# An adaLN block with a mixture of experts: blocks of four sizes at the end, and a first chunk in two halves

## The chip, the cores and the metric

The kernel runs on one core of a Trainium2 chip. The metric is the device time of one execution in microseconds (us). A core has five engines that run their own instruction streams side by side: TensorE (PE in the profile; its weight loads are the row PEld), VectorE (DVE), ScalarE (ACT), GpSimd (POOL) and SyncE (SP), which here only issues transfers. They wait for each other through semaphores. All data is float32.

## The reference, cut to what matters

There are T = 4 x 1024 = 4096 tokens of D = 256 features. A modulation `mod`, one row of six parts for each of the four sequences, scales and shifts two layer norms and gates two residual branches. The first branch is a gated scan along the sequence, the second a mixture of 8 experts of which every token uses two.

```python
mod = (silu(c) @ wmod).reshape(4, 6, 1, 256)
sa, ca, ga, sb, cb, gb = (mod[:, i] for i in range(6))
ga, gb = at_least_a_quarter(ga), at_least_a_quarter(gb)     # keeps the sign
h = layernorm(x) * (1 + ca) + sa
# branch 1
xn = rms_scale * h / (norm(h) * 256 ** -0.5 + 1e-8) * split_scale
K = sigmoid(xn @ W_K)                                        # 256 -> 512
u, g_in, g_out = split(xn @ W_ugg, 3)                        # 256 -> 3 x 512
u = u * sigmoid(g_in) * (1 - K)
s = scan(s_t = K_(t-1) * s_(t-1) + u_t)                      # along the sequence
x = x + ga * ((s * sigmoid(g_out)) @ W_out + h)
# branch 2
h = layernorm(x) * (1 + cb) + sb
w = two best of softmax(h @ Wg + bg), scaled to sum 1
y = sum over the two experts e of
      w_e * (gelu(h @ W1[e] + b1[e]) @ W2[e] + b2[e])        # 256 -> 1024 -> 256
x = x + gb * y
```

## The kernel before, in words

The order of the instructions on every engine is written out by hand (the tile framework runs in manual schedule): what a function emits first is queued first, and each engine works its queue in order.

**The start** (lines 95 to 165, 200 to 312 and 988 to 1019). SP's queue takes `c`, then a third of `wmod`, the other two thirds, W_K, three parts of W_ugg, the second chunk of x, W_out and the third chunk. ACT's queue takes the first chunk of x (512 tokens, four tiles of 128), then the small vectors, `rms_sb` and `split_sb` among them. VectorE takes the mean and variance of the first chunk (`stats`, line 213; the power -0.5 on GpSimd), `shift` (226), ScalarE normalizes (`norm`, 232). TensorE multiplies a broadcast silu(c) with the first third of `wmod` into the bank `pm` (989). VectorE applies `1 + ca` and `sa` to the four tiles (996). ScalarE sums the squares (`a_square`, 364), `a_root` (375) and `a_scale` (380) make `u`, the tokens divided by their rms. TensorE turns `u` (1014), and ScalarE and VectorE, one half of the features each, bring it out of PSUM as `hT`, multiplied by `rs_sb`, the product of the two scale vectors (1015, 1016). `all_rows` (287) meanwhile makes the modulation of all four sequences, which `other_rows` (299) finishes and stores in DRAM as `rows`; from there later chunks read theirs as `mda` and `mdf`. `keep_busy(n)` (260) puts n transposes of the identity into TensorE's queue, whose result nothing reads; it is called with 14, 8 and 18.

**Stage A** (loop at line 1020) works through eight chunks of TB = 512 tokens. Each chunk has four calls of `project` (402), one for each 128 of the 512 columns, and each of these four products `pk`, `pgi`, `pu` and `pgo` of two matmuls over all 512 tokens (417), in four PSUM banks. The vector work of the previous and the next chunk is laid between them. After the scan comes the output projection (`o_pe`, 446), the second layer norm, and the gate (`f_gate`, 554): its weights are padded to 32 columns so that four products stand side by side in TensorE's columns. VectorE then picks the two best experts, and GpSimd scatters each token's number and weight to a list of its expert in DRAM (`drain`, 582).

**Stage B** works through blocks of TK = 256 entries of these lists. `b_up(j)` (917) multiplies the block's tokens `xT` by W1 (16 matmuls into banks `ph`, GELU by ScalarE into `g`), `b_down(j)` (952) multiplies `g` by W2, 128 tokens at a time into a bank `py` of eight matmuls; VectorE adds the bias and scales the rows (972, 973), and GpSimd adds them to their places in the output by an indirect DMA (`add_rows`, 944). `b_turn(j + 1)` (898) turns the next block's gathered rows on VectorE, between the two; it is 16 transposes of 32x32 squares, over two tiles or, with `half`, over one. Entries are fetched three blocks ahead, rows (gathers by GpSimd) and weights (two transfers of 1 MB) two ahead; weights lie in three places, of which every third is `proj` (line 114), once the projections' weights. While the routing is not complete, blocks come from partial tables; at block 8 VectorE makes the last table (`late_table`, 765, out of `blocks_of`, 700, and `table`, 709), which puts blocks of at most 128 tokens last.

Whatever the routing, at least 28 blocks are whole and at least 32 exist; these bounds are `sure_whole` and `sure`. So blocks 2 to 27 are emitted without a branch. Blocks 28 to 31 are a branch each, whole or half (128 tokens). From block 32 on, `rest` (1202) nests: if block j exists, add what the previous one kept, do block j, go on with j + 1, up to `NJ` = 39 possible blocks. A block from 31 on keeps its last part back in `last_y` and `last_at`, and the add comes at the start of the next `rest` or at the end:

```python
    def work_either(j, keep=False):
        with tc.If(n_whole > j) as whole:
            work(j, False, keep)
        with whole.Else():
            work(j, True, keep)

    def rest(j):
        with tc.If(n_blocks > j):
            add_rows(last_y, last_at, T)
            work_either(j, True)
            if j + 1 < NJ:
                rest(j + 1)
```

## Time and profile before

| | |
|---|---|
| median of the runs (3) | 790.62 us (790.05 to 791.95) |
| the profiled execution's own time | 789.1 us |
| its span, first to last instruction | 787.4 us |
| granted TensorE clock, mean | 0.997 |
| TensorE busy | 772.8 us (98%) |
| VectorE, ScalarE, GpSimd busy | 504.3, 241.7, 290.3 us |
| TensorE busy in 0 to 30 us | 27.82 us |
| TensorE busy in 30 to 400, 400 to 728 us | 368.06, 327.33 us |
| TensorE busy in 728 us to the end | 49.60 of 59.40 us |
| DMA share in 400 to 728 us | 0.81, 227 GB/s |

How to read the lines that the profile gives: L928 is line 928 of the kernel. A group's row names the line, the engine and the operation, then the tiles (output, then inputs), their shapes, and how many such instructions it holds; in a timeline two columns stand ahead, the start in us from the start of the span and the busy time, and in square brackets the idle time before the group with what ended it. `ph_False` and `pye_False` are the PSUM banks of a whole block's two products, `ph_True` and `pye_True` those of a half one. A matmul of float32 has two records here and a transpose one, so 16 matmuls are 32 records. Busy times come from the profiled execution alone.

### The profile page before, as it was taken

How to read it: one execution, taken by the hardware profiler on the slowest of the kernel's cores; microseconds unless marked ns; L12 is line 12 of the kernel's file. 1: busy time of each engine (PE TensorE's matmuls, PEld its weight loads, DVE VectorE, ACT ScalarE, POOL GpSimd, SP SyncE). 2: the span in 40 equal slices, each digit the busy share in tenths (PEclk: the TensorE clock that was granted, in tenths of full speed). 3: DMA queues.
4: the chain of work that ended last, by engine and by line, in shares of the span. 5: the costliest groups of instructions: out<-in, count | busy, mean ns of one | idle time of the engine just before them, and what ended most of it. 6: DMA issues, size and time to landing. Idle time of an engine off the chain costs nothing.

```text
span 787.4 us, 10804 instructions
## 1 busy us (share of the span) xinstructions
PE 772.8 (98%) x3279; PEld 577.1 (73%) x3279; DVE 504.3 (64%) x1391; ACT 241.7 (31%) x560; POOL 290.3 (37%) x370
## 2 busy tenths in 40 slices
PE   8999999999999999999999999999999999999995
PEld 5455545454546557888888888888888888888994
DVE  5787877898789869767547453544536354453563
ACT  4434243534433343223222122221312222131231
POOL 2102010106142712456564564634434243343431
PEclk9999999999999999999999999999999999999998
DMA  8321334042313265799469898898878687885781
GB/s 296 95 70 47 116 102 142 23 127 86 100 55 113 55 185 183 241 328 258 73 161 206 249 247 253 245 294 223 235 211 230 186 235 217 218 232 167 221 264 25
DMA packets 116040, 138.13 MB, mean 175 GB/s; under 512 B 25782, under 2 KB 100090, under 8 KB 115968
## 3 DMA queue, kind: packets, MB, share of 16 engines
q1 hardware_dynamic: 97184, 111.46, 45.0%
q0 software_dynamic: 17216, 25.25, 15.9%
q10 hardware_dynamic: 1568, 0.57, 0.3%
q8 instruction: 32, 0.52, 0.3%
q14 instruction: 40, 0.33, 0.1%
HBM read 113.52 MB, written 25.42 MB: 176 GB/s over the span
## 4 chain that ended last, share of the span: by engine, by line
PE 83%; DMA 8%; DVE 4%; issue 2%; POOL 1%; ACT 1%; POOLq 0%; DVEq 0%
PE ph_False L928 25%; PE pye_False L958 23%; PE pya L454 7%; PE pk L417 6%; PE pgi L417 6%; PE pu L417 6%; PE pgo L417 6%; DMA hb<-hx,ent 5%; DMA out_dram<-yb_False,ent 2%; PE idle L263 1%; DMA proj<-in_L_ffn_W_dram 1%; PE pm L290 1%; PE pta L399 1%; PE pl L564 1%; DVE s L443 0%
## 5 line engine op out<-in xcount | busy, mean ns | idle before, releaser
L937 ACT ACTIVATE g_False<-ph_False,bb 128x256 f32<-128x256 f32 x248 | 103.8, 470 | 303.0 <-issue 188.2
L915 DVE STREAM_TRANSPOSE xT<-hb 32x128 f32<-32x128 f32 (+1 forms) x576 | 168.8, 293 | 12.7 <-DMA hb<-hx,ent 3.6
L958 PE MATMUL pye_False<-w,g_False 128*128 128x256 f32 x672 | 148.7, 379 | 0.0
L928 PE MATMUL ph_False<-xT,w 128*128 128x256 f32 x672 | 148.6, 379 | 0.0
L928 PEld LDWEIGHTS ph_False<-xT,w 128*128 128x128 f32 x672 | 127.4, 190 | 17.9 <-issue 0.7
L958 PEld LDWEIGHTS pye_False<-w,g_False 128*128 128x128 f32 x672 | 127.5, 190 | 17.6 <-issue 0.2
L945 POOL DMA_INDIRECT out_dram<-yb_False,ent x46 | 73.4, 1595 | 139.9 <-DVE yb_False L973 138.4
L972 DVE TENSOR_TENSOR yb_False<-pye_False,b2b 128x256 f32<-128x256 f32 x42 | 17.8, 424 | 126.3 <-PE pye_False L958 123.8
L586 POOL DMA_INDIRECT lists<-pay,placei x64 | 66.4, 1037 | 38.5 <-DMA ent<-lists 27.4
L928 PE MATMUL ph_False<-xT,proj 128*128 128x256 f32 x320 | 70.8, 379 | 0.7 <-DMA proj<-in_L_ffn_W_dram 0.7
L958 PE MATMUL pye_False<-proj,g_False 128*128 128x256 f32 x320 | 70.7, 379 | 0.0
L928 PEld LDWEIGHTS ph_False<-xT,proj 128*128 128x128 f32 x320 | 60.7, 190 | 9.3 <-DVE yb_False L972 1.0
L958 PEld LDWEIGHTS pye_False<-proj,g_False 128*128 128x128 f32 x320 | 60.8, 190 | 8.3
L830 POOL DMA_INDIRECT hb<-hx,ent x53 | 55.6, 1048 | 22.4 <-issue 15.6
L417 PE MATMUL pk<-hT,proj 128*128 128x512 f32 x128 | 61.0, 599 | 0.7 <-ACT hT L1015 0.7
L223 POOL TENSOR_TENSOR rstd_f<-rstd_f,expo 128x4 f32<-128x4 f32 x8 | 8.2, 1022 | 142.4 <-DVE rstd_f L222 98.8
L417 PE MATMUL pu<-hT,proj 128*128 128x512 f32 x128 | 60.2, 592 | 0.0
L417 PE MATMUL pgo<-hT,proj 128*128 128x512 f32 x128 | 60.2, 592 | 0.0
L417 PE MATMUL pgi<-hT,proj 128*128 128x512 f32 x128 | 60.2, 592 | 0.0
L454 PE MATMUL pya<-wo,z 128*128 128x256 f32 x256 | 56.8, 380 | 0.0
L454 PEld LDWEIGHTS pya<-wo,z 128*128 128x128 f32 x256 | 48.4, 190 | 8.6 <-issue 2.4
L972 DVE TENSOR_TENSOR yb_False<-pye_False,wo_sb 128x256 f32<-128x256 f32 x20 | 8.5, 424 | 60.4 <-PE pye_False L958 60.3
(234 smaller groups left out, 811.1 us busy)
## 6 DMA issues: line engine op xcount, KB each, us to landing
w<-in_L_ffn_W_dram SPq DMA_DIRECT2D x48, 1024.0 KB
proj<-in_L_ffn_W_dram SPq DMA_DIRECT2D x24, 1024.0 KB
hx<-gb SPq DMA_DIRECT2D x4, 1024.0 KB
out_dram<-x SPq DMA_DIRECT2D x8, 512.0 KB
hx<-h SPq DMA_DIRECT2D x8, 512.0 KB
x<-in_L_attn_x_dram SPq DMA_DIRECT2D x7, 512.0 KB
swapped<-u SPq DMA_DIRECT2D x7, 512.0 KB
hT<-swapped SPq DMA_DIRECT2D x28, 128.0 KB
```

Of the source, the lines that this page charges most:

```text
L223: nc.gpsimd.tensor_tensor(rstd, rstd, expo[:, 0, :], ALU.pow)
L263: nc.tensor.transpose(idle[:, :P], ident, ident)
L417: nc.tensor.matmul(ps, lhsT=w[:, k, col : col + P], rhs=hT[:, k, :], start=(k == 0), stop=(k == KC - 1),)
L454: nc.tensor.matmul(py[:, t, :], lhsT=z[hc][:, ts(2 * q + t, P)], rhs=wo[:, hc, :], start=(hc == 0), stop=(hc == HC - 1),)
L586: ins = nc.gpsimd.indirect_dma_start(out=lists[:, :], out_offset=IndirectOffsetOnAxis(ap=place, axis=0), in_=what, in_offset=None, bounds_ ...
L830: nc.gpsimd.indirect_dma_start(out=hb[:, t, :], out_offset=None, in_=hx[: seen(j), :], in_offset=IndirectOffsetOnAxis(ap=BK[j]["ent"][:, t ...
L915: nc.vector.transpose(to[ts(q, SQ), :, :, ts(i, SQ)], hb[ts(i, SQ), :, :, ts(q, SQ)])
L928: nc.tensor.matmul(ph[:, u, :], lhsT=w1[:, k, ts(fc, P)], rhs=xT[:, k, :n], start=(k == 0), stop=(k == KC - 1),)
L937: nc.scalar.activation(g[:, fc, :n], ph[:, u, :], AF.Gelu_apprx_tanh, bias=bb[:, fc : fc + 1])
L945: return nc.gpsimd.indirect_dma_start(out=out_rows[:n], out_offset=IndirectOffsetOnAxis(ap=at, axis=0), in_=yb, in_offset=None, bounds_che ...
L958: nc.tensor.matmul(py, lhsT=g[:, fc, ts(t, P)], rhs=w2[:, fc, :], start=(fc == 0), stop=(fc == FC - 1),)
L972: nc.vector.tensor_add(yb, py, b2b)
```

## The change

**Sizes of blocks.** Blocks have one of four sizes, 256, 192, 128 and 64, instead of two. `late_table` counts, for each expert, how many blocks reach into each size, and puts all of one size before those of the next. For each size a count `n_upto` is loaded into registers. The bounds are worked out for each size (`sure(k)`): 26 blocks are whole in any case, 32 exist. So blocks 26 to 31 and the nested ones from 32 on choose among those sizes that are possible for their number, by branches inside each other's Else. Rows are fetched and turned in tiles of 128 as before (`half` is `size <= P`). The product up takes as many columns as the size; the product down takes the last part with 64 rows if the size leaves 64: its eight matmuls then go in turn to the lower and the upper 64 output partitions of the same bank, and VectorE adds the two halves of the bank with one more instruction. `last_y` is cleared once at the start by GpSimd, since a kept part of 64 rows is added with all 128. A temporary of the last table lies in the W_out tile.

**The first chunk.** Its first 256 tokens come by ACT's queue, the other 256 by SP's between the first and the second part of `wmod`. Statistics, normalization, modulation, squares, root, scaling and the turn are made for two tiles at a time. The first call of `project` makes its four products for the first 256 tokens, then turns the second half (ahead of the fourth product), then makes the four products of the second half into the same banks; `other_rows`, `load_mdf(0)`, the statistics of chunk 1 and its `shift` stand behind the second turn, in the middle of that call. The copies of silu(c) transposed, `scT` and its broadcast `scB`, go from VectorE to ScalarE, behind two transfers that ACT issues. The product `rs_sb` stands earlier on VectorE. The three copies of `all_rows` stand behind the first turn on ScalarE. `keep_busy` is called with 10 and 4, and no third time.

The core of the diff:

```diff
+    HT = TPB // 2
+    halves = [slice(i * HT, (i + 1) * HT) for i in range(2)]
+    X[0] = {"x": deep.tile([P, TPB, D], F32, tag="x", name="x_0", bufs=5)}
+    x0 = x[0].rearrange("(n p) d -> p n d", p=P)
     nc.sync.dma_start(out=c_sb, in_=c)
-    load_x(0, nc.scalar)
+    nc.scalar.dma_start(out=X[0]["x"][:, halves[0]], in_=x0[:, halves[0]])
     nc.sync.dma_start(out=wmod_sb[:, :, : 2 * D], in_=wmod_r[:, :, : 2 * D])
+    nc.sync.dma_start(out=X[0]["x"][:, halves[1]], in_=x0[:, halves[1]])
     nc.sync.dma_start(out=wmod_sb[:, :, 2 * D :], in_=wmod_r[:, :, 2 * D :])
...
+    def new_stats(what: str):
...
+    def stats_of(xb, tiles, at):
+
+        st, mv, rstd = tiles
+        for n in range(at.start, at.stop):
             nc.vector.bn_stats(st[:, n, :], xb[:, n, :])
-        for n in range(TPB):
+        for n in range(at.start, at.stop):
             nc.vector.bn_aggr(mv[:, n, :], st[:, n, :])
-        nc.vector.tensor_scalar_add(rstd, mv[:, :, 1], LN_EPS)
-        nc.gpsimd.tensor_tensor(rstd, rstd, expo[:, 0, :], ALU.pow)
-        return mv, rstd
-
-    def shift(c_):
+        nc.vector.tensor_scalar_add(rstd[:, at], mv[:, at, 1], LN_EPS)
+        nc.gpsimd.tensor_tensor(rstd[:, at], rstd[:, at], expo[:, 0, at], ALU.pow)
...
-    keep_busy(14)
+    keep_busy(10)
     pt = ps_tr.tile([P, TB], F32, tag="tr", name="pt_c")
     for k in range(KC):
         nc.tensor.transpose(pt[:, k * B : (k + 1) * B], sc[:, ts(k, P)], ident[:B, :B])
-    nc.vector.tensor_copy(scT.rearrange("p k b -> p (k b)"), pt[:, : KC * B])
-
-    scB = setup.tile([P, KC, P], F32, tag="scB", name="scB")
-    nc.vector.tensor_copy(scB, scT[:, :, 0:1].broadcast_to((P, KC, P)))
-    keep_busy(8)
-    mda = deep.tile([P, 2, D], F32, tag="mda", name="mda_0")
     with nc.allow_non_contiguous_dma(reason="a few hundred elements, once"):
         nc.scalar.dma_start(out=rms_sb, in_=rms_scale.rearrange("(k p) -> p k", p=P))
         nc.scalar.dma_start(out=split_sb, in_=split_scale.rearrange("(k p) -> p k", p=P))
+    nc.scalar.copy(scT.rearrange("p k b -> p (k b)"), pt[:, : KC * B])
+
+    scB = setup.tile([P, KC, P], F32, tag="scB", name="scB")
+    nc.scalar.copy(scB, scT[:, :, 0:1].broadcast_to((P, KC, P)))
+    keep_busy(4)
+    mda = deep.tile([P, 2, D], F32, tag="mda", name="mda_0")
     nc.scalar.dma_start(out=b1_sb, in_=b1.rearrange("e (c p) -> (e c) p", p=P))
     nc.scalar.dma_start(out=wg_sb[:, :, :E], in_=Wg.rearrange("(k p) e -> p k e", p=P))
     nc.scalar.dma_start(out=bg_sb, in_=bg.rearrange("(o e) -> o e", o=1).broadcast_to((P, E)))
-    X[0]["stats"] = stats(X[0]["x"], "a0")
-    shift(0)
-    a_norm(0)
+    tiles0 = new_stats("a0")
+    X[0]["stats"] = tiles0[1:]
+    X[0]["h"] = deep.tile([P, TPB, D], F32, tag="h", name="h_0")
+    for at in halves:
+        stats_of(X[0]["x"], tiles0, at)
+    for at in halves:
+        shift(0, at)
+        norm(X[0]["h"], 0, at)
...
-        nc.scalar.copy(rows_sb[:, 2 * i : 2 * i + 2, :].rearrange("b r d -> b (r d)"), pm[:B, :])
+        row_parts.append(pm)
+
+    def all_rows_copied():
+        for i, pm in enumerate(row_parts):
+            nc.scalar.copy(
+                rows_sb[:, 2 * i : 2 * i + 2, :].rearrange("b r d -> b (r d)"), pm[:B, :]
+            )
...
-            ps = ps_mm.tile([P, TB], F32, tag="mm", name=f"p{what}_{c_}_{hc}")
+        def product(w, col, what, at=slice(0, TB), ps=None):
+            if ps is None:
+                ps = ps_mm.tile([P, TB], F32, tag="mm", name=f"p{what}_{c_}_{hc}")
             for k in range(KC):
                 nc.tensor.matmul(
-                    ps,
+                    ps[:, at],
                     lhsT=w[:, k, col : col + P],
-                    rhs=hT[:, k, :],
+                    rhs=hT[:, k, at],
                     start=(k == 0),
                     stop=(k == KC - 1),
                 )
             return ps
 
-        ps = product(wk_sb, hc * P, "k")
+        args = {
+            "k": (wk_sb, hc * P), "gi": (wu_sb, H + hc * P), "u": (wu_sb, hc * P),
+            "go": (wu_sb, 2 * H + hc * P),
+        }
+        if halved is None:
+
+            def out_of(what):
+                return product(*args[what], what)
+        else:
+
+            half, done = TB // 2, {}
+            for what in args:
+                if what == "go":
+                    halved()
+                done[what] = product(*args[what], what, slice(0, half))
+
+            def out_of(what):
+                return product(*args[what], what, slice(half, TB), done[what])
...
-        past = small.tile([P, n, sg], F32, tag="past", name=f"past{what}", bufs=1)
+        if what == "l":
+            past = wo_sb.rearrange("p c d -> p (c d)")[:, D : D + n * sg]
+            past = past.rearrange("p (n s) -> p n s", s=sg)
+        else:
+            past = small.tile([P, n, sg], F32, tag="past", name=f"past{what}", bufs=1)
...
+    QT = P // 2
+    sizes = [TK, TK - QT, P, QT]
+    NS = len(sizes)
...
+        upto = [
+            blocks_of(float(TK - 1 - (sizes[k + 1] if k + 1 < NS else 0)), f"l{k}")
+            for k in range(NS)
+        ]
+        for k in range(NS):
+            nc.vector.tensor_sub(counts4[:, k, :], upto[k], upto[k - 1] if k else done)
+        for k in range(1, NS):
+            nc.vector.tensor_add(
+                starts[:, k * E : (k + 1) * E], starts[:, (k - 1) * E : k * E],
+                counts4[:, k - 1, :],
+            )
...
-        n = P if half else TK
-        at_once = TB // n
+        at_once = min(TB // n, FC // 2)
...
-            py = ps_y.tile([P, D], F32, tag="y", name=f"pye_{j}_{t}_{half}")
+        parts = [(0, min(size, P))] + ([(1, size - P)] if size > P else [])
+        for t, n in parts:
+            py = ps_y.tile([P, D], F32, tag="y", name=f"pye_{j}_{t}_{size}")
+
+            beside = P // n
             for fc in range(FC):
                 nc.tensor.matmul(
-                    py,
-                    lhsT=g[:, fc, ts(t, P)],
+                    py[ts(fc % beside, n), :],
+                    lhsT=g[:, fc, ds(t * P, n)],
                     rhs=w2[:, fc, :],
-                    start=(fc == 0),
-                    stop=(fc == FC - 1),
+                    start=(fc < beside),
+                    stop=(fc >= FC - beside),
                 )
...
+            nc.vector.tensor_add(yb[:n], py[:n], b2b[:n])
+            if beside > 1:
+                nc.vector.tensor_add(yb[:n], yb[:n], py[n:])
...
     last_y = xpool.tile([P, D], F32, tag="last_y", name="last_y", bufs=1)
+    nc.gpsimd.memset(last_y, 0.0)
...
+    def first_mod(n: int):
         nc.vector.scalar_tensor_tensor(
             h[:, n, :], pm[:, D:], 1.0, h[:, n, :], ALU.add, ALU.mult
         )
         nc.vector.tensor_add(h[:, n, :], h[:, n, :], pm[:, :D])
-    a_square(0)
+
+    for n in range(HT + 1):
+        first_mod(n)
+    a_square(0, halves[0])
+    a_root(0, halves[0])
+    nc.vector.tensor_mul(rs_sb, rms_sb, split_sb)
+    for n in range(HT + 1, TPB):
+        first_mod(n)
+    a_square(0, halves[1])
     nc.scalar.copy(mda[:, 0, :], pm[:, :D])
-    a_root(0)
+    a_scale(0, halves[0])
+    a_root(0, halves[1])
     nc.vector.tensor_scalar_add(mda[:, 1, :], pm[:, D:], 1.0)
-    nc.vector.tensor_mul(rs_sb, rms_sb, split_sb)
     for i in range(6 * D // TB):
         all_rows(i)
-    keep_busy(18)
-    a_scale(0)
...
+    def first_turn(i: int):
+        at = slice(i * HT * P, (i + 1) * HT * P)
+        for t in range(i * HT, (i + 1) * HT):
+            for k in range(KC):
+                nc.tensor.transpose(pts[k][:, ts(t, P)], X[0]["u"][:, t, ts(k, P)], ident)
+        nc.scalar.activation(hT[:, 0, at], pts[0][:, at], AF.Copy, scale=rs_sb[:, 0:1])
+        nc.vector.tensor_scalar_mul(hT[:, 1, at], pts[1][:, at], rs_sb[:, 1:2])
+
+    first_turn(0)
+    all_rows_copied()
+    a_scale(0, halves[1])
...
-        project(c_, 0, [lambda: a_norm(nxt)] if more else [])
+        project(
+            c_, 0, [lambda: a_norm(nxt)] if more else [],
+            None if c_ else lambda: (
+                first_turn(1), other_rows(), load_mdf(0), a_stats(1), shift(1)
+            ),
+        )
...
+    def sure(k: int):
+
+        less = sizes[k + 1] if k + 1 < NS else 0
+        return (
+            (2 * T - E * less) // TK,
+            max((2 * T - p * (less + 1)) // TK + p for p in range(E + 1)),
+        )
+
+    def work(j: int, size: int, keep: bool):
+        fetch_used(j, size <= P)
+        b_up(j, size)
         if j + 1 < NJ:
 
-            b_turn(j + 1, half)
-        b_down(j, half, keep=keep)
-
-    def work_either(j: int, keep: bool = False):
-        with tc.If(n_whole > j) as whole:
-            work(j, False, keep)
-        with whole.Else():
-            work(j, True, keep)
-
-
-    sure_whole = (2 * T - E * P) // TK
-    sure = 2 * T // TK
+            b_turn(j + 1, size <= P)
+        b_down(j, size, keep=keep)
+
+    def work_any(j: int, keep: bool):
+
+        able = [
+            k for k in range(NS) if j < sure(k)[1] and (k == 0 or j >= sure(k - 1)[0])
+        ]
+
+        def choose(i: int):
+            k = able[i]
+            if i == len(able) - 1:
+                work(j, sizes[k], keep)
+                return
+            with tc.If(n_upto[k] > j) as first:
+                work(j, sizes[k], keep)
+            with first.Else():
+                choose(i + 1)
+
+        choose(0)
+
+    sure_whole, sure_any = sure(0)[0], sure(NS - 1)[0]
+    assert sure(NS - 1)[1] == NJ
...
+    n_upto = [
+        nc.values_load(
+            ends_at[0:1, k : k + 1], min_val=sure(k)[0], max_val=NJ,
+            skip_runtime_bounds_check_because=why,
+        )
+        for k in range(NS)
+    ]
+    n_blocks = n_upto[-1]
+    for j in range(sure_whole, sure_any):
+        work_any(j, j == sure_any - 1)
 
     def rest(j: int):
         with tc.If(n_blocks > j):
             add_rows(last_y, last_at, T)
-            work_either(j, True)
+            work_any(j, True)
```

## The prediction

> **What bounds the kernel now.** I read the page first, then the timeline of TensorE alone, then those of VectorE and GpSimd over the last 30 us.
>
> ```profile
> span 787.4 us, 10804 instructions
> ...
> PE 772.8 (98%) x3279; PEld 577.1 (73%) x3279; DVE 504.3 (64%) x1391; ACT 241.7 (31%) x560; POOL 290.3 (37%) x370
> ```
>
> TensorE is busy for 772.8 of 787.4 us. Its timeline shows where most of the other 14.6 lie: 1.5 before the first instruction, 0.67 before the first projection, 0.67 at block 8 and 9.8 after the last matmul. The span therefore moves by what TensorE's own work shrinks, by when it reaches the first `pk`, and by what follows its last matmul.
>
> ```profile
> 8.94 5.31 PE L290 MATMUL pm<-wmod_sb,scT 128*4 128x512 f32 x12
> 14.18 2.19 PE L263 MATMUL idle<-ident 128*128 128x128 f32 x18
> 16.21 1.04 PE L1014 MATMUL pta<-ident,u 128*128 128x128 f32 x8
> 17.91 1.98 PE L417 MATMUL pk<-hT,proj 128*128 128x512 f32 x4 [0.67 <-ACT hT L1015]
> ...
> 728.26 7.07 PE L928 MATMUL ph_False<-xT,w 128*128 128x256 f32 x32
> 735.16 7.07 PE L958 MATMUL pye_False<-w,g_False 128*128 128x256 f32 x32
> 742.07 3.73 PE L928 MATMUL ph_True<-xT,w 128*128 128x128 f32 x32
> 745.64 3.62 PE L958 MATMUL pye_True<-w,g_True 128*128 128x256 f32 x16
> 749.10 3.73 PE L928 MATMUL ph_True<-xT,proj 128*128 128x128 f32 x32
> ```
>
> Columns: start, busy time, then the group. From start to start a 256-token block takes 6.90 up and 6.91 down, a 128-token block 3.57 up and 3.46 down. The work before 17.91 is a chain through all engines, with TensorE filled by idle transposes.
>
> **Which blocks run.** The counts of `ph_False` (672+320 records, 32 a block) and `ph_True` (96+64) give 31 whole and 5 half blocks. Routing the given inputs by the reference gives the experts 1849, 1836, 484, 383, 1127, 837, 1258 and 418 tokens; beyond multiples of 256 that is 57, 44, 228, 127, 103, 69, 234 and 162. With four sizes it becomes 30 whole, one of 192 (the 162), three of 128, two of 64 (57 and 44). Still 36 blocks: only blocks 30, 34 and 35 shrink.
>
> **The 192 block.** Up has 32 records, whose cost runs between 3.57 (N=128) and 6.90 (N=256): 5.24, a gain of 1.67. Down is one part of 128 rows (3.46) and one of 64, whose eight products now go to two halves of the output partitions in turn. No 64-wide row exists; the nearest is the gate product, four 32-wide column tiles.
>
> ```profile
> 95.88 0.65 PE L564 MATMUL pl<-hT,wg_sb 128*32 128x128 f32 x16
> 96.45 1.99 PE L417 MATMUL pk<-hT,proj 128*128 128x512 f32 x4
> ```
>
> Sixteen 128-column records, at 0.11 each 1.8 us one after another (32 `ph_True` take 3.57), are over in 0.57: tiles run side by side, all but fourfold. Two tiles give 3.46/2 = 1.73; the bounds are 1.73 and 3.46. A rule speaks against it: the Trainium skill, TensorEngine Tiling (Array Packing), Key Properties, says that changing the tiling mode drains TensorE. The gate row has a 0.33 idle weight queue before it; I charge 0.25 for the mode in and out. Gain down: 3.45-1.73-0.25, about 1.4. Without drain it would be 1.7. The block: **-3.0**, ends -1.4 and -3.4.
>
> **The 64 blocks on TensorE.** Up does not shrink. With N=64 and even N=8 these weight loads keep their pace:
>
> ```profile
> 395.28 0.30 PEld L676 LDWEIGHTS pr<-earlier,ones 128*128 128x128 f32 x2
> 395.50 0.30 PEld L680 LDWEIGHTS pr<-ended,ones 128*128 128x128 f32 x2
> 395.72 0.95 PEld L928 LDWEIGHTS ph_False<-xT,w 128*128 128x128 f32 x5
> ```
>
> Two records take 0.22, the 0.11 each of N=128. So up stays 3.57; down is 1.73+0.25: about 5.5 instead of 7.03. GELU of 64 columns costs no more than the 0.25 a step of 128 and follows.
>
> **The 64 blocks on VectorE** decide. Each turn still handles a 128-row tile (half is `size <= P`), and `last_y`, of which there is one, waits for the previous add to land.
>
> ```profile
> 764.55 0.15 DVE L968 COPY last_at<-ent 128x1 int32<-128x1 int32 x1 [1.35 <-DMA out_dram<-last_y,last_at]
> ...
> 765.64 4.00 DVE L915 STREAM_TRANSPOSE xT<-hb 32x64 f32<-32x64 f32 x16
> 770.16 0.15 DVE L968 COPY last_at<-ent 128x1 int32<-128x1 int32 x1 [0.52 <-DMA out_dram<-last_y,last_at]
> ...
> 771.57 4.00 DVE L915 STREAM_TRANSPOSE xT<-hb 32x64 f32<-32x64 f32 x16
> 775.66 0.15 DVE L968 COPY last_at<-ent 128x1 int32<-128x1 int32 x1
> ...
> 778.09 0.48 DVE L973 SCALAR_TENSOR_TENSOR last_y<-last_y,ent,hb 128x256 f32<-128x256 f32 x1
> ```
>
> In the clock of before (block 30's gain set aside): block 34 starts at 763.30 and would end near 768.8, but xT of block 35 is ready only at 769.64, since its turn starts at 765.64. TensorE waits 0.9; block 35 runs 769.75 to 775.2. VectorE: block 34's end starts at about 769.9 (turn over, add of 33 landed), takes 1.06 (764.55 to 765.61) plus one more add of 0.46: 771.4. Turn of 36, made though no such block exists: 771.5 to 775.5. Block 34's add starts at 771.7 on GpSimd and lands after 3.83 (771.83 to 775.66): 775.5. Block 35's end: 775.6 to 777.1, where before had 778.57. **-1.4**; bounds 0 (no column overlap) and -3.1 (TensorE sets the end). Weights do not decide: the second half of block 35's, issued at 761.90, had landed by 768.9, and block 35's down starts 773.3.
>
> **The branches.** Before, eight blocks (28 to 35) take a jump each; now blocks 26 to 35 take about 19 in nests of two to four. The trace shows branch instructions of 0.07 to 0.45 us on TensorE's sequencer, which runs some 3.4 us ahead of the array at the end of a half block; block to block the array stops nowhere but 0.36 at 763. A rule speaks against: the Trainium skill, Runtime: NRT & Kernel Launch, Instruction fetch mechanics: a taken branch out of the fetched window waits for a DMA. The trace's 16 KB instruction fetches take mostly 0.9 to 1.4 us; by the rule 11 more jumps could cost 12 us, by the row nothing. I take the row for TensorE and **+0.3** for VectorE in the last two blocks, where it has no such lead; bounds 0 and +12. Not-taken branches also make GpSimd raise DMA semaphores, 1.4 us each; for block 35 its two remaining variants have equal DMA counts, so it does not get worse.
>
> **The start.** The first chunk arrives as 256 KB on ACT's queue, the rest behind the first third of `wmod` on SP's (0.4 us more issue there, pushing `wmod`'s rest and W_K; the first projection's weights landed by 11.1, its `u` by 14.2, `go` by 15.6). Step by step: with 10 and 4 idle transposes scT and scB (ACT now, behind two DMA issues that end at 4.03) are ready at 5.1 instead of 5.6; `pm` starts when its weights land, 5.4 to 6.2 (before 6.75), and ends near 8.2. ACT is free of its DMA issues at 6.9, so norm of the first half is 6.9 to 7.9, before 8.82 to 10.89 for all. Three first_mod of 0.79 each: 8.5 to 10.9. Squares, root and pow (1.0) of the first half: 12.0. New wait: the product rs_sb now stands ahead of the fourth first_mod, and `split` landed at 12.14; with half a chunk ahead of it I put it at 11.6. VectorE queues first_mod 3 and a_scale behind it: u of the first half at 13.9, after all_rows (12 records of 0.43, ended 13.2). Four transposes 0.5, hT of 256 columns 0.45: `pk` at 15.1. The bank of `pm` is free at 14.8, so it just holds. Project (0,0) is then 8 half products of 0.86 and 0.5 of transposes: ends 22.5 against 24.89, **-2.4**. Its costs: other_rows (3.1) and a_stats(1) (1.9) start on VectorE after the second hT, at 18.9, so shift(1) comes at 25.2 (24.06 before), `nu` and a_norm later, and `pgo` of the next project waits 0.3 for its bank. Net **-2.1**, ends 0 and -3.2. The three row copies (0.48 each) move on ACT behind the first hT and are over at 17.0, before the second; the store of `rows` moves on SP from 21.2 to 22.3, ahead of mdf and the fourth chunk, whose first reader, a_skip, comes in the fourth projection, after 38. The 18 removed transposes leave TensorE idle for about 0.7 us, no cost. That it carries: TensorE stops for 0.67 at block 8 on weights that were issued after lists whose scatters follow TensorE's own results, so it moves along.
>
> **At nothing.** The last table: four passes of 0.54 double, some fourteen small operations of 0.18 are added, about +5 us on VectorE at block 8, from 435.0 to 440. It delays `yb`; the next `py` needs its bank at 445.08, so 4 us of cover remain. Memset of last_y: GpSimd at its start.
>
> **Sum.** -3.0 -1.4 +0.3 -2.1 = -6.2. The profiled execution took 789.1 (span 787.4, 1.7 around it): 782.9. The median of the runs, 790.62, is 1.5 higher: **784.4**.
>
> **Rivals.** (1) Column tiles of 64 don't overlap: block 30 keeps its 1.7 up and pays the drain, the 64 blocks give nothing; -1.4-2.1+0.3: 787.4. For: no such row; against: the gate row. (2) The start gives nothing because late `split` or a bank stalls what was won: 786.5. For: VectorE is in order; against: the idle transposes from 14.18 to 16.1 are pure waiting, and the first `pk` now waits for half a chunk only. (3) VectorE does not hold the 64 blocks and the start gives all: -3.0-3.1-3.0+0.3: 781.8. (4) Slower: jumps between variants miss the fetched instructions. It decides when the 11 added jumps cost 0.56 us uncovered each; at 1.1 each 790.6-6.2+12 = 796. For: code grows to four variants a block; against: the sequencer's lead. (5) The change doesn't do what it says, all remainders falling into old sizes: excluded by the counts.
>
> **Chances.** Mine 0.55, (1) 0.12, (2) 0.15, (3) 0.1, (4) 0.08. The measurement tells about 0.3%, 2.4 us. (2), (3) and mine are faster, so is most of (1) at -3.2; a part of it and of small fetch losses lands within 0.3%: faster 0.84, same 0.09, slower 0.07. The range takes in (1) to (3) and leaves out (4) and the outer tails: 781.4 to 788.4. Mine alone: 783.0 to 786.0.
>
> **What would show it.** First `pk` near 15.1 and second project's `pk` near 22.5; a 192 group with `ph` of 5.2 and a 64-row `pye` of 1.7 to 2.0; in the 64 blocks `ph` still 3.5; a wait for xT before block 35; the last GpSimd add 1.4 us closer to block 31's start than the 36.9 of before (742.07 to 778.93). Wrong it would be if 64-row `pye` took 3.4, or if TensorE had gaps of 1 us at block starts from 26 on.

## The result, and the profile after

The changed kernel takes 799.08 us (median of 4 runs, 794.72 to 803.91) against 790.40 (4 runs, 790.05 to 791.95): a ratio of 1.0109, 95% interval 1.0082 to 1.0136. It is 1.1% slower; 784.4 was forecast. Its runs also spread over 9 us, those of before over 2: from the fastest on, the four had a mean granted clock of 0.992, 0.988, 0.988 and 0.980, and 0.012 of 799 us is 9.6 (an estimate).

The profiled execution took 800.62. First its page, three lines:

```profile
span 798.9 us, 10892 instructions
...
PE 770.7 (96%) x3269; PEld 574.3 (72%) x3269; DVE 509.1 (64%) x1411; ACT 240.8 (30%) x563; POOL 290.7 (36%) x373
...
PEclk9999999999999999999999999999999999999897
```

TensorE is busy for 2 us less than before, and the span is 11.5 longer. Part of that busy time was at a lower clock: the last row shows digits under 9 at the end. Where the time went is in TensorE's timeline (start, busy time, group, and in brackets the idle time before it):

```profile
16.84 1.13 PE L448 MATMUL pk<-hT,proj 128*128 128x256 f32 x4 [0.46 <-ACT hT L1097]
...
24.29 1.88 PE L448 MATMUL pk<-hT,proj 128*128 128x512 f32 x4
...
453.29 7.14 PE L994 MATMUL ph<-xT,w 128*128 128x256 f32 x32 [0.47 <-DMA w<-in_L_ffn_W_dram]
...
468.40 7.14 PE L994 MATMUL ph<-xT,proj 128*128 128x256 f32 x32 [1.06 <-DVE yb L1045]
...
731.27 5.44 PE L994 MATMUL ph<-xT,w 128*128 128x192 f32 x32 [0.18 <-issue]
736.54 5.49 PE L1028 MATMUL pye<-w,g 128*128 128x256 f32 x32
744.65 5.44 PE L994 MATMUL ph<-xT,w 128*128 128x128 f32 x32 [2.61 <-issue]
...
755.74 5.44 PE L994 MATMUL ph<-xT,proj 128*128 128x128 f32 x32 [2.20 <-issue]
...
764.47 3.73 PE L994 MATMUL ph<-xT,w 128*128 128x128 f32 x32
...
773.89 4.90 PE L994 MATMUL ph<-xT,w 128*128 128x64 f32 x32 [2.23 <-issue]
778.72 3.68 PE L1028 MATMUL pye<-w,g 128*64 128x256 f32 x16
...
786.39 1.95 PE L1028 MATMUL pye<-proj,g 128*64 128x256 f32 x16
```

Read it against before in stages. The second project's `pk` is 0.6 us earlier than in this trace of before (24.29, 24.89), but no earlier than in the six later traces with the old start (24.27 to 24.45). Block 8 is 0.66 later (424.95, 424.29): 0.9 us were lost in front of the gate at 280 us, waiting for the transfer that brings its `hT`, and block 8's own wait for weights grew from 0.67 to 0.90. Block 10 is 1.30 later (453.29, 451.99), block 11 2.6 later (468.40, 465.81). The row at 468.40 names VectorE, which ended just then; the landings in the trace have block 11's first weights at 468.26, and that is the wait. Block 30 is 3.0 later (731.27, 728.26). From there the new sizes do what they should: block 30 lasts from 731.27 to 742.03, 10.76 where 10.7 was forecast. But in front of blocks 31, 32 and 34 TensorE stands still for 2.61, 2.20 and 2.23 us with nothing to wait for ("issue"), and the blocks that follow are slow: the same 32 records of `ph` at 128 columns take 5.44 at 744.65 and 3.73 at 764.47.

Two more views explain both. The first lists what one source line issued, here its branches (count, shortest/median/longest in ns). These are TensorE's branches of before, at the nest's `if block j exists`, and of the changed kernel, at the choice of a size:

```profile
L1203 PEldq COMPARE_BRANCH  x6: 65/68/3697, 747.0 to 779.3; - x6
```

```profile
L1258 PEldq COMPARE_BRANCH  x25: 65/225/3262, 673.6 to 779.9; - x25
```

Most branches take a quarter of a microsecond or less. Four at the choice of a size take 2.9 to 3.3 us (starts 727.41, 740.76, 752.17, 770.19), one more at the very end 3.96. During each of them the trace has a 16 KB instruction fetch (at 741.65 for the second), which itself takes 0.9 to 1.2 us. Before, there was one such branch, 3.70 at the end, where it delays nothing.

The second view gives stretches of time: length, busy time of each engine with its instructions, granted clock, DMA share, GB/s.

```profile
742.13:745.54 3.41, 0.89 (x8) 0.93 (x9) 2.44 (x8) 0.00 (x0) 2.50 (x4) 1.00 0.92 323
745.54:748.95 3.41, 3.41 (x19) 3.41 (x18) 2.76 (x13) 1.14 (x4) 1.06 (x1) 0.50 1.02 282
...
776.26:783.09 6.83, 6.83 (x33) 4.82 (x32) 1.83 (x8) 1.54 (x8) 0.00 (x0) 0.50 0.02 3
```

The engines stand in the order PE, PEld, DVE, ACT, POOL. The first row holds most of the stop before block 31: TensorE works for 0.89 of its 3.41 us, still at full clock (1.00). In the second the clock is 0.50. Within 2.4 us of the end of each of the three stops the clock is halved: from 745.54 for 3.41 us, from 755.78 for 3.41 and from 776.26 for 6.83. That costs half of 13.65, so 6.8 us (an estimate: TensorE is the bound there), on top of the 7.0 of the stops. The tail thus pays 13.8 us and saves some 5.6 (from block 30's start, 3.0 late, to the last add, 790.15 against 778.93 and so 11.2 late, it loses 8.2).

### The profile page after: what moved, and what is told of

Its sections match the earlier page's. It is cut to its first block, busy times and chain, and to the rows that moved or that the text cites. A ratio compares the mean times of both kernels' runs of the same rounds, so it can differ in the third digit from the quotient of the medians.

```text
span 798.9 us, 10892 instructions
## 1 busy us (share of the span) xinstructions
PE 770.7 (96%) x3269; PEld 574.3 (72%) x3269; DVE 509.1 (64%) x1411; ACT 240.8 (30%) x563; POOL 290.7 (36%) x373
## 4 chain that ended last, share of the span: by engine, by line
PE 37%; DMA 27%; issue 17%; POOL 8%; DVE 7%; POOLq 1%; ACT 1%; SPq 0%; another core or an unknown queue 0%; ACTq 0%; DVEq 0%
DMA out_dram<-yb,ent 15%; PE pk L448 5%; POOL out_dram L1012 5%; PE pya L504 5%; PE ph L994 5%; PE pgi L448 5%; PE pgo L448 5%; PE pu L448 5%; DMA lists<-pay,placei 5%; PE pye L1028 4%; DMA ent<-lists 3%; DMA out_dram<-last_y,last_at 2%; POOL lists L637 1%; DMA wmod_sb<-in_L_wmod_dram 1%; DVE s L493 1%
## 5 line engine op out<-in xcount | busy, mean ns | idle before, releaser
L1003 ACT ACTIVATE g<-ph,bb 128x256 f32<-128x256 f32 (+3 forms) x288 | 114.0, 451 | 343.7 <-issue 214.4
L994 PE MATMUL ph<-xT,w 128*128 128x256 f32 (+3 forms) x768 | 161.2, 369 | 5.5 <-issue 5.0
L1028 PE MATMUL pye<-w,g 128*128 128x256 f32 (+1 forms) x720 | 158.0, 385 | 0.0
L994 PEld LDWEIGHTS ph<-xT,w 128*128 128x128 f32 x768 | 140.2, 195 | 24.1 <-issue 7.7
L1028 PEld LDWEIGHTS pye<-w,g 128*128 128x128 f32 (+1 forms) x720 | 133.2, 190 | 19.9 <-issue 1.5
L1012 POOL DMA_INDIRECT out_dram<-yb,ent x46 | 73.2, 1592 | 135.9 <-DVE yb L1045 133.9
L994 PE MATMUL ph<-xT,proj 128*128 128x256 f32 (+2 forms) x384 | 80.4, 370 | 4.2 <-issue 2.2
L994 PEld LDWEIGHTS ph<-xT,proj 128*128 128x128 f32 x384 | 69.9, 197 | 14.2 <-issue 4.6
L1028 PE MATMUL pye<-proj,g 128*128 128x256 f32 (+1 forms) x352 | 76.3, 379 | 0.0
L1028 PEld LDWEIGHTS pye<-proj,g 128*128 128x128 f32 (+1 forms) x352 | 64.8, 188 | 9.1
```

The lines of the kernel that those rows point to most:

```text
L994: nc.tensor.matmul(ph[:, u, :], lhsT=w1[:, k, ts(fc, P)], rhs=xT[:, k, :n], start=(k == 0), stop=(k == KC - 1),)
L1003: nc.scalar.activation(g[:, fc, :n], ph[:, u, :], AF.Gelu_apprx_tanh, bias=bb[:, fc : fc + 1])
L1012: return nc.gpsimd.indirect_dma_start(out=out_rows[:n], out_offset=IndirectOffsetOnAxis(ap=at, axis=0), in_=yb, in_offset=None, bounds_che ...
L1028: nc.tensor.matmul(py[ts(fc % beside, n), :], lhsT=g[:, fc, ds(t * P, n)], rhs=w2[:, fc, :], start=(fc < beside), stop=(fc >= FC - beside),)
```

## The experiments

Each time stands beside that of the kernel before on the same chip. Chips differ (before took 788.61 to 790.74), so ratios count more than medians.

**The parts apart: tail alone, start alone, jumps alone, table alone.** The first two are the diff's two halves, each on the kernel before. In the third, the code and the branches are those of all four sizes, but the table rounds so that 31 whole and 5 half blocks are taken, as before:

```diff
-            blocks_of(float(TK - 1 - (sizes[k + 1] if k + 1 < NS else 0)), f"l{k}")
-            for k in range(NS)
+            blocks_of(float(P - 1 if k < 2 else TK - 1), f"l{k}") for k in range(NS)
```

The fourth puts this table, as long as the changed one, into the kernel before, whose branches and blocks it keeps.

> Only the four sizes with their branches and table; the start is that of before. Theory J (far jumps on TensorE and the longer table cost the time): TensorE has branches of 2.9 to 4 us at about four block starts from 30 on, gaps of 2.2 to 2.6 us each, half clock after them, and block 11 waits for weights: 799 to 802 us, since the start alone gave only 0.6. Rival, the start is part of the loss: 794 or less.

> Only the first chunk in two halves; two sizes as before. If what the trace of the changed kernel shows carries over: second project's pk at 24.3 against 24.89 before, ScalarE's issue of wg_sb held until 9.8 and its normalization until 10.8, and a wait of 0.9 in the gate at 280: 789.5 to 791. Rival, the start as forecast (-2.1): 788.3.

> The start of before; the code of all four sizes and their branches, but the table rounds up so that only blocks of 256 and 128 are ever taken (31 and 5, as before). Theory J: the same long branches at four or so block starts, so 790.4 + 2.4 for the table + 12 to 16 for stalls and clock: 803 to 808. Rival S (the new shapes cause the gaps: 64-row column tiles, 192 columns): no gap over 0.5 at block starts, 790.4 + 2.4 = 793.

> Before, with the last table made over four sizes of which two are empty: 5 us more on VectorE at block 8, and nothing else (same blocks, same branches). If the table delays the weights by way of GpSimd's queue and SP's: waits at blocks 10 and 11 of 1.5 to 2.4 us in sum, 792 to 793. If the weights of block 11 were late for another reason: 790.4, within 0.3 us.

Measured, against 788.61 of before: tail alone 799.63 (ratio 1.0149, 1.0118 to 1.0180), start alone 790.90 (1.0018, 0.9999 to 1.0037), jumps 798.41 (1.0116, 1.0096 to 1.0137), table alone 791.08 (1.0039, 1.0021 to 1.0056).

So the loss is the tail's, and it is there without any block of a new size. Jumps and table without new sizes cost 9.8 us, less than the 803 to 808 that I had expected; in the trace only one of its stops was followed by half clock. The table alone costs 2.5, so the branches cost about 7.3. The trace of the jumps agrees: its span is 10.8 us longer than before's, of which the stops are 7.2, the half clock (3.41 us of it) 1.7 and the wait for block 10's weights 1.65. TensorE's branches and timeline with the jumps alone:

```profile
L1190 PEldq COMPARE_BRANCH  x26: 65/184/5422, 671.6 to 786.1; - x26
```

```profile
753.83 3.81 PE L942 MATMUL ph<-xT,proj 128*128 128x128 f32 x32 [2.92 <-issue]
...
772.37 5.44 PE L942 MATMUL ph<-xT,w 128*128 128x128 f32 x32 [4.25 <-issue]
```

The rival that the new shapes cause the gaps is out: these are the old shapes. With the table alone, block 10 waits:

```profile
452.77 7.14 PE L943 MATMUL ph_False<-xT,w 128*128 128x256 f32 x32 [1.79 <-DMA w<-in_L_ffn_W_dram]
```

The way there can be followed in the queues. The table holds VectorE, whose last steps of block 8 come late; GpSimd's add of them starts at 439.39 (436.26 before, in a trace in which block 8 itself began 1.2 us later), and with it, in order, the scatter to the lists behind it (441.30 against 438.17). SP's next load of entries, which waits for that scatter, is issued at 444.51 (443.10 before), and block 10's weights stand behind it on SP's queue.

**The start's holds.** In the changed kernel ScalarE normalizes the first chunk at 10.83, where 6.9 was forecast (and 8.82 measured before). Its queue:

```profile
5.26 0.53 ACTq L296 DMA_DIRECT2D b_sb<-in_L_ffn_b_dram  x1
9.83 0.37 ACTq L297 DMA_DIRECT2D wg_sb<-in_L_ffn_Wg_dram  x1
...
10.83 2.07 ACT L253 ACTIVATE h<-x,nmr,rstd_a 128x256 f32<-128x256 f32 x4 [5.98 <-DMA rms_sb<-in_L_attn_rms_scale_dram]
```

The program marks the landing of transfers with eight semaphores in turn, and a transfer is issued only when the one that had its semaphore before has landed. With one transfer more at the start, the turn moves by one: `wg_sb` now gets the semaphore of `wmod`'s second part, which lands at 9.75 (before: that of the first chunk, landed by 4.9). ScalarE stands behind its own issue. The row at 10.83 names `rms_sb` because the next issue, `bg_sb`, waits for that one's semaphore, which had landed at 9.95. The second hold is the one that the prediction had counted, `rs_sb` waiting for `split_sb` ahead of other work on VectorE. The first try moves the three small transfers behind the normalization, the second puts the idle transposes back, the third moves the transfers to SP's queue and the product behind the first half's scaling:

```diff
     for at in halves:
         shift(0, at)
         norm(X[0]["h"], 0, at)
+    nc.scalar.dma_start(out=b1_sb, ...); nc.scalar.dma_start(out=wg_sb, ...); nc.scalar.dma_start(out=bg_sb, ...)
```

```diff
         all_rows(i)
+    keep_busy(18)
```

```diff
-    nc.scalar.dma_start(out=b1_sb, ...); nc.scalar.dma_start(out=wg_sb, ...); nc.scalar.dma_start(out=bg_sb, ...)
+    nc.sync.dma_start(out=b1_sb, ...); nc.sync.dma_start(out=wg_sb, ...); nc.sync.dma_start(out=bg_sb, ...)
...
-    nc.vector.tensor_mul(rs_sb, rms_sb, split_sb)
...
     a_scale(0, halves[0])
+    nc.vector.tensor_mul(rs_sb, rms_sb, split_sb)
```

> The first chunk in halves alone, with ScalarE's three small transfers (b1_sb, wg_sb, bg_sb) issued after its normalization instead of before. If the hold of wg_sb's issue until 9.8 is what ate the gain of the start: normalization of the first half at 6.9 to 7.9 instead of 10.8, first pk at 15.0 to 15.6, second project's pk at 22.4 to 23.0: 2.1 less than the kernel before, 786.5. Rival, it isn't that hold (split_sb or the banks of the modulation come late): pk at 16.8 or later, no less than the run without this edit.

> The first chunk in halves alone, with the 18 idle transposes behind the modulation put back. If the 2.3 us that TensorE stands still there costs a half clock afterwards (3.4 us of it in the profiled run of the first chunk alone, so 1.7 us): no stretch of half clock in the first 30 us, and about 1.5 less than that run, 789.0 to 789.5. If the half clock came by chance: the same as that run, 790.5 to 791.

> The first chunk in halves alone, with the three small transfers on SP's queue behind the third chunk instead of on ScalarE's, and the product rs_sb behind the scaling of the first half. If both holds (ScalarE's queue on a transfer slot, VectorE on split_sb) are what was left: squares of the first half start by 10.5 instead of 12.8, first pk at 14.6 to 15.4, second project's pk at 22.2 to 22.9; 788.3 to 788.9 if the kernel before takes 790.7. Rival, the next thing late takes its place: pk at 16 or later, no less than before.

Measured: 790.81 against 790.74 (1.0002, 0.9990 to 1.0015), 791.80 against 790.74 (1.0011, 0.9999 to 1.0022), and 788.16 against 789.67 (0.9984, 0.9975 to 0.9994). The first was a miss of mine: normalization does start at 7.83, but now the same three issues stand ahead of the squares, the last until 12.73, and `pk` starts at 16.72. The idle transposes give nothing in the time, though in their trace the first 30 us are at full clock. The half clock that the trace of the start alone shows at 17.4 to 20.8 does not come every time: the changed kernel has the same stop of 2.29 us there and no half clock. With both holds gone the forecast of the start comes true in the trace (first and second project's `pk`):

```profile
14.45 1.13 PE L448 MATMUL pk<-hT,proj 128*128 128x256 f32 x4 [0.46 <-ACT hT L1076]
...
21.89 1.88 PE L448 MATMUL pk<-hT,proj 128*128 128x512 f32 x4
```

Traces with the start of before have 24.27 to 24.89 for the second of these; of the 2.4 to 3.0 us, 1.5 remain in the time.

**The table placed later.** The kernel with the table alone, its table behind block 8's product down:

```diff
-        elif j == NE:
-            tab["l"], ends_at = late_table()
         b_down(j, mid=lambda: drain(1))
+        if j == NE:
+            tab["l"], ends_at = late_table()
```

> The kernel before with the long last table, emitted behind block 8's product down instead of ahead of it. If the table delays block 10's and 11's weights because it holds VectorE's last step of block 8, and with it GpSimd's and SP's queues: no wait for weights at block 10, the time of before, 788.6 within 0.6. Rival, the table delays something else (the transposes of block 10, the entries): still 1 us or more at block 10 and 790.5 to 791.

Measured 795.57 against 790.74 (1.0073, 1.0047 to 1.0099): worse, and the rival was right. The table now stands ahead of the transposes of block 10:

```profile
454.34 7.17 PE L943 MATMUL ph_False<-xT,w 128*128 128x256 f32 x32 [1.74 <-DVE xT L930]
```

VectorE's free time between a block's turn and its first `yb` is some 5 us, and the table takes 9.4: it fits nowhere in one piece.

**How far a jump may go.** In the kernel before, code that never runs, of growing length, ahead of blocks 18 to 25 (the counts of blocks are loaded into registers at block 17 for it):

```diff
+        if j in skipped:      # {18: 32, 19: 64, 20: 96, 21: 128, 22: 160, 23: 192, 24: 256, 25: 320}
+            with tc.If(n_blocks > NJ - 1):
+                for i in range(skipped[j]):
+                    nc.tensor.transpose(dead[:, :P], ident, ident)
```

> The kernel before with code that never runs ahead of blocks 18 to 25: behind a branch, 32, 64, 96, 128, 160, 192, 256 and 320 transposes of TensorE (64 of them are as many TensorE instructions as a whole block). Theory J: the branch over 32 and 64 takes TensorE 0.2 to 0.5 us, the branch over some 128 or more 2.6 to 3.7 us, all of it or all but a few tenths covered by the sequencer's lead of 3.4 us: 789 to 793. Rival, a long branch is a matter of nested branches and not of the code skipped: all eight under 0.5 us.

A single execution took 798.32 us, more than the 789 to 793 expected: the eight stops behind the branches are 4.4 us, and half clock from 651.74 for 3.41 us adds 1.7. The eight branches of TensorE, in order, take 0.37, 0.32, 0.31, 0.31, 0.31, 0.41, 5.83 and 4.04 us:

```profile
L1185 PEldq COMPARE_BRANCH  x8: 313/343/5834, 558.4 to 662.5; - x8
```

```profile
650.76 8.83 PE L928 MATMUL ph_False<-xT,w 128*128 128x256 f32 x32 [2.13 <-PEq L1185]
...
666.83 7.14 PE L928 MATMUL ph_False<-xT,w 128*128 128x256 f32 x32 [0.33 <-PEq L1185]
```

So it is length and not nesting, as far as one jump of each length can tell: a plain branch over 192 transposes is short, one over 256 long. My limit of 128 was too low for a single jump out of a long block. In the nests two jumps follow each other closely, over the rest of one block's variants and over the first ones of the next, and they stall at less: counted in TensorE's and its weight queue's records (128 for a whole block, 96 for one of 128 tokens; 512 for the 256 transposes), 320 to 448 skipped records stalled ahead of blocks 30, 31, 32 and 34 of the changed kernel and 224 ahead of block 33 did not; in the run of jumps alone 224 stalled once. What exactly decides, such as where the code lies in its 16 KB pages, stays open. A stall is hidden as far as the sequencer is ahead: behind whole blocks the 4.04 left no more of a gap than the short ones do (0.33), the 5.83 left 2.13.

**Pieces.** The four sizes with the start of before, each late block branching twice, and the table in three parts at blocks 8, 9 and 10; then this with the mended start; then also two `last_y` in turn, and one tile of rows fetched where a block has at most 128:

```diff
-        choose(j, ks, work)
+        choose(j, [k for k in ks if sizes[k] > QT] or ks, up)          # product up alone
+        choose(j, ks, turn_and_down)                                   # b_turn(j + 1), b_down(j)
...
-            tab["l"], ends_at = late_table()
+            next(late)      # one of three parts, also at NE + 1 and NE + 2
```

```diff
-                yb, at = last_y, last_at
+                yb, at = parted[j % 2]
...
         with tc.If(n_blocks > j) as more:
-            add_rows(last_y, last_at, T)
+            add_rows(*parted[(j - 1) % 2], T)
             work_any(j, True)
             ...
+        with more.Else():
+            add_rows(*parted[(j - 1) % 2], T)
```

> The four sizes with the start of before; each late block branches twice, once around the product up (three variants, 64 tokens take that of 128) and once around the turn and the product down, so that each branch skips less code; the last table is made in three parts at blocks 8, 9 and 10. Theory J: no TensorE branch over 1 us before the last, no gap over 0.6 at block starts, no wait for weights at block 10: the forecast of the tail after all, -3.0 for block 30 and -1 to -3 for the two blocks of 64: 785 to 787.5 if the kernel before takes 790.7. Rival, more branches cost more wherever they are: gaps at block starts again, 792 or more.

> The last two together. If they add: 2 us less than the run in pieces alone, 783 to 785.5. If the start's gain is lost on the way (waits for weights at block 8 or in the gate at 280 take it): the same as the run in pieces.

> The last two together, with two pairs of last_y and last_at in turn, and one tile of rows fetched instead of two where a block has at most 128 tokens. In the two runs in pieces VectorE waits 2 to 3 us for the landing of the add before last, and for the gather of the second tile, at blocks 33 to 35. If these waits are what holds the two blocks of 64: no gap over 1 us before blocks 32 to 35, the half clock at the end gone, 2 to 5 us less than both together, 783 to 786 if the kernel before takes 789.7. Rival, VectorE's own work (4.0 of transposes, 1.5 of scaling) holds them: 787, as before this edit.

Measured: pieces 788.64 against 789.67 (0.9988, 0.9975 to 1.0002), with the start 787.27 (0.9966, 0.9953 to 0.9979), with two `last_y` 785.00 against 788.77 (0.9951, 0.9937 to 0.9964). In pieces the longest branch at the choice is 1.03 us and no wait of half a microsecond is left at blocks 8 to 11. The branches and the table were mended together; what each gave was not measured apart. With the mended start one branch takes 2.19 again (741.95) and TensorE stops for 1.13 before block 32, so shorter branches made the stalls rarer and did not end them. The gain was less than forecast (some 1 us and 2.4 where 3.2 to 5.7 and 5.2 to 7.7 were expected), and the trace of pieces shows the next holder, VectorE:

```profile
760.45 3.84 PE L956 MATMUL ph<-xT,w 128*128 128x128 f32 x32 [0.95 <-DVE xT L940]
...
769.10 5.32 PE L956 MATMUL ph<-xT,proj 128*128 128x128 f32 x32 [2.93 <-DVE last_at L1000]
```

With two buffers the second of these waits is 1.63 (none over 1 was expected), and in the profiled execution no half clock comes before the last matmul. In others it probably did: 6 of the 22 had a mean clock of 0.991 to 0.994, where the profiled one had 0.997, and the four slowest (787.99 to 789.6) are among them. The last kernel beats before by 3.8 us, and the changed one by more. Its remaining waits end with the gather of the next rows:

```profile
765.22 4.00 DVE L991 STREAM_TRANSPOSE xT<-hb 32x64 f32<-32x64 f32 x16 [2.13 <-DMA hb<-hx,ent]
```

## Why the prediction was wrong

**The branches, +0.3: the step that failed.** They cost about 7.3 us (jumps less table), and in the changed kernel's trace 7.0 of stops with 6.8 of half clock behind them; rival (4), the jumps that miss the fetched instructions, is what happened, and 796 was near. That is in part luck: it summed 11 jumps at 1.1 us each, where three stops of 2.2 to 2.6 came, with half clock behind each, and 2.5 us of the table that it had at nothing. Two readings failed in it. "The trace shows branch instructions of 0.07 to 0.45 us" left out the one of 3.70 in the same trace, at the end, where it delays nothing. It was the only row that showed a jump over much code, and so the row to price the new jumps by. The 0.9 to 1.4 of an instruction fetch, which I took instead, is a third of the stall. And the lead of 3.4 us was read at the end of a half block: at 740.76, after the 64-row products and two short branches, the array had only 1.3 us left. The rule that I weighed against it, in the Trainium skill, Runtime: NRT & Kernel Launch, Instruction fetch mechanics, was right in kind.

**The clock.** No step had a price for standing still. Each stop of over 2 us in the changed kernel's tail was followed by half clock: 6.8 us. The Trainium skill, TensorE: Matmul & The Clock Gate, Part 1, has windows of some 3.4 us and half rate after an idle one. The lengths agree (3.41, 3.41, 6.83), but no window had to be idle. In all 14 traces the recorded clock changes only at whole steps of 3.413 us, counted from where the full clock begins (in before's, 774.83 us of full clock are 227 steps). Up to the last matmul, ten steps at full clock hold 1.38 us of TensorE's work or less, and half clock follows each. Of those with 1.67 or more it follows one alone, the 2.37 us ahead of 776.26, in which 64-column products ran; why there stays open. So it counts how much of a stop falls into one step. The stop of 2.92 in the run of jumps alone was divided between two, with 2.04 and 1.86 us of work left, and the clock stayed full:

```profile
748.87:752.28 3.41, 2.04 (x10) 1.46 (x8) 0.91 (x2) 0.00 (x0) 0.10 (x1) 1.00 0.34 113
752.28:755.69 3.41, 1.86 (x16) 1.89 (x17) 2.73 (x12) 0.00 (x0) 2.56 (x2) 1.00 0.64 164
```

The steps begin elsewhere in each execution, so the same stop is followed by half clock in one and not in another.

**The last table, at nothing.** It costs 2.5 us. The size was nearly right (in the changed kernel 9.5 on VectorE against 5.5, so 4.0 more where 5 was forecast), the cover was not: I asked when TensorE next needs the bank that `yb` frees, and 4 us were left there. What was late first was GpSimd's queue behind `yb`, then SP's, then weights of block 10. That is the wait behind a wait that the step should have followed.

**The start, -2.1.** 0.6 against the profiled run of before, nothing against the other traces with the old start, nothing that the time can tell. "ACT is free of its DMA issues at 6.9" failed: it was 10.7, for want of a semaphore. The rest of the chain was sound: with the holds gone `pk` comes at 14.45 (15.1 forecast) and the second project at 21.89 (22.5).

**The 192 and the 64 blocks.** The block of 192 took 10.76 (10.7). The eight products of 64 rows in two column halves took 1.95 at full clock (1.73 + 0.25 forecast), and `ph` at 64 columns still 3.72 from start to start in the run of the tail alone (3.57 forecast): both near enough, and rival (1) is out. In the changed kernel VectorE did not hold the 64 blocks, because TensorE's stops came first; in pieces it does, for 2.93, where 0.9 was forecast, since the turn waits for the landing of the add before (1.94) and then for its rows (1.48).

## What to carry to other kernels

A branch is priced by the code that it skips on the engine with most instructions, summed over jumps that follow closely, and the longest branch anywhere in a trace gives a first price even where it delays nothing there. Where TensorE may stand still for 2 us or more, the half clock that can follow belongs in the sum. What is put into an engine's free time has to be followed through every queue that waits for that engine, one after the other, and not only to the bound's next need. Where a transfer is added near the start, look at which engine's next issue it holds.

## What the runs showed of the hardware that was not expected

A jump of TensorE over too much code takes 2.6 to 5.8 us, and a single one over 192 transposes 0.41. A stop of 2 us can cost as much again in half clock. Whether it comes is not settled by the length of the stop (2.20 and 2.23 were followed by it, 2.92 was not), but in ten of eleven cases by the work left in one step of 3.413 us: 1.38 us or less brought it, 1.67 or more did not.
